# Layer-norm variance on GpSimd, and a different share of the depthwise convolution on TensorE, in a float32 transformer block

## The chip, the cores and the metric

The kernel runs on one core of a Trainium2 chip. The core has five engines that run side by side, each with its own queue of instructions: TensorE (PE in the profile; PEld is its loading of weights), VectorE (DVE), ScalarE (ACT), GpSimd (POOL) and SyncE (SP, used here to issue transfers). Transfers are carried out by 16 DMA engines; GpSimd, ScalarE and SyncE can issue them, and some transfers add to what lies at their target ("accumulating" transfers). The metric is the time of one execution on the device in microseconds (us).

## The reference, cut to what matters

The input is a batch of 16 images with 128 channels and 96 x 96 pixels, all in float32. One block of a Restormer-like network is computed: a layer norm over channels, attention between channels, a second layer norm, and a feed-forward part with a 3 x 3 depthwise convolution on 512 hidden channels.

```python
B, C, H, W = (16, 128, 96, 96)
HEADS = 8; HID = 4 * C; EPS = 1e-05

def _layernorm(x, w, b):
    mu = jnp.mean(x, axis=-1, keepdims=True)
    var = jnp.mean(jnp.square(x - mu), axis=-1, keepdims=True)
    return (x - mu) / jnp.sqrt(var + EPS) * w + b

def _ffn(xn_nchw, w_in, w_dw, w_out):
    h1 = einsum('bchw,oc->bohw', xn_nchw, w_in[:, :, 0, 0])
    h2 = conv_general_dilated(h1, w_dw, strides (1, 1), padding ((1, 1), (1, 1)), feature_group_count=HID)
    h3 = gelu(h2, approximate=False)
    return einsum('bchw,oc->bohw', h3, w_out[:, :, 0, 0])

xn1 = _layernorm(x_hwc, ln1_w, ln1_b)              # over the 128 channels of a pixel
x = x + attention(xn1, wq, wk, wv, wp)             # softmax over channels, 8 heads of 16
xn2 = _layernorm(x_hwc, ln2_w, ln2_b)
x = x + _ffn(xn2, w_in, w_dw, w_out)
```

## The kernel before

Channels lie on the 128 partitions, pixels along the free dimension. An image is cut into 8 bands of 12 rows (1152 pixels), a band into 3 units of 4 rows (384 pixels); there are 128 bands, numbered g. The 512 hidden channels are 4 chunks of 128, numbered n.

The order of instructions on every engine is fixed when the program is built. The kernel describes each operation with an engine, a place in time, its inputs and outputs and an estimated duration; a small planner then simulates the engines and writes the instructions down in the order in which they would start. The table `AT` shifts the place of each kind of operation, and so acts as a table of priorities.

```python
PE_CHUNK = 3
PE_BANDS = (0, 2, 4, 6, 8, 10)
PE_OF = 11
PE_LAST = (0, 1, 2, 4, 5, 7)
DMA_TAPS = (1, 2, 3)
QT, QB = 4, 1
X1_BUFS, XB_BUFS, PR_BUFS, H3_BUFS, ZT_BUFS = 2, 6, 5, 10, 3
AT = dict(weights=10.45, ..., stats_a=-5.05, variance_a=-7.4, power_a=-1.65, shift_a=-5.8, ...)
```

A layer norm over channels needs pixels on the partitions, so each group of four tiles of 128 pixels is transposed into a PSUM bank (two such banks, `p_tr`, take turns; at the start of the program other banks are used), and what follows happens there. The variance, the power and the shift work on 4 numbers per partition:

```python
def forth(q):                     # TensorE: 4 transposes into one PSUM bank
    ... nc.tensor.transpose(d["pT", q][:, k, :], xt[:, j * P : (j + 1) * P], ident)

def stats(j):                     # VectorE: mean and squared deviations, two tiles at a time
    nc.vector.bn_stats(d["st"][:, j, :], d["pT", qs[h]][:, k : k + 2, :].rearrange("p t c -> p c t"))

def variance():                   # 128 x 4
    nc.vector.tensor_scalar(ve, d["mv"][:, :, 2], 1.0 / C, EPS, ALU.mult, ALU.add)

def power():                      # GpSimd: (var + eps) ** -0.5, 128 x 4
    nc.gpsimd.tensor_tensor(rstd, d["ve"], mhalf, ALU.pow)

def shift():                      # VectorE: -mean * rstd, 128 x 4
    nc.vector.scalar_tensor_tensor(nb, d["mv"][:, :, 1], -1.0, d["rstd"], ALU.mult, ALU.mult)

def scaled(q):                    # ScalarE: normalised tile into SBUF, one per tile of 128 pixels
    nc.scalar.activation(zT(q)[:, k, :P], d["pT", q][:, k, :], AF.Identity, bias=nb, scale=rstd)
```

The first norm (`_a`) feeds the gram matrix of the channels on TensorE, from which attention is worked out; both norms then transpose back (`pB_a`, `pB_b`) and place the result in `xn`. An image has 72 tiles, or 18 groups of four, for each norm: 288 groups of the first norm and 288 of the second in the whole program.

The depthwise convolution is shared out. For a pair (g, n) in `jobs`, TensorE makes the hidden rows, ScalarE copies them out of PSUM and multiplies them for tap 0 and for two or three more taps, whose products are summed by accumulating transfers that GpSimd issues; VectorE does the other five or six taps, one instruction each over the whole band:

```python
def product(t):                   # ScalarE
    nc.scalar.activation(to, shifted(t), AF.Copy, scale=dw[:, n, t : t + 1])

def tap(t):                       # VectorE, 128 x 1152: two tensor inputs and a scalar
    nc.vector.scalar_tensor_tensor(h3, shifted(t), dw[:, n, t : t + 1], h3, ALU.mult, ALU.add)

def add_products(t):              # issued by GpSimd
    nc.gpsimd.dma_start(out=to, in_=d["pr", t], accum_op=ALU.add)
```

The fourth chunk (n = 3) of some bands is done by TensorE alone instead: the hidden layer's weights are multiplied into the nine taps (`comp`), and nine matmuls per unit add up in PSUM, three units to a band; then ScalarE applies the gelu. Which bands these are:

```python
def by_pe(g):
    k = NG - 1 - g
    return k in PE_LAST if k < NB else k % PE_OF in PE_BANDS

jobs += [(g, n) for n in range(NCH) if n != PE_CHUNK or not by_pe(g)]
```

At last `ffn_out` multiplies the four chunks with the output weights and VectorE adds the result to x. The weights themselves are transposed once, in the opening, at the place `weights`.

Of the kernel before, what the change touches and what calls it, by code (L numbers as in the profile page):

```python
# [11 lines left out]
ALU = mybir.AluOpType  # L12
# [4 lines left out]
EPS = 1e-5  # L17
UR = 4
BR = 12
PE_CHUNK = 3  # L20
PE_BANDS = (0, 2, 4, 6, 8, 10)
PE_OF = 11
PE_LAST = (0, 1, 2, 4, 5, 7)
TINY = 1e-20
DMA_TAPS = (1, 2, 3)
# [4 lines left out]
X1_BUFS, XB_BUFS, PR_BUFS, H3_BUFS, ZT_BUFS = 2, 6, 5, 10, 3  # L30
IN_TURN = ("tr", "h3", "pr", "xb", "x1")
AT = dict(
    weights=10.45, zeros=-0.55, load_a=-15.15, forth_a=-12.6, stats_a=-5.05, variance_a=-7.4,
    power_a=-1.65, shift_a=-5.8, scaled_a=-2.25, gram=-2.15, back_a=-19.55, place_a=-30,
    attention=-11.35, mix=-10.3, residual=-15.8, mixed=-15.6, add_x=2.25, forth_b=-11.95, stats_b=-3.7,
    variance_b=-5.4, power_b=-20.6, shift_b=-22.65, scaled_b=-2.4, back_b=-19.15, place_b=-0.55,
    halo=4.55, hidden=-1.65, kept=-8.9, product=-7.6, products=2.05, add_last=-4.65, tap=7.3,
    add_first=25.4, gelu=-4.85, conv=-0.8, conv_gelu=-6.2, out=2.3, add=7.1, store=-8.95,
)
STEP = dict(scaled=0.3, hidden=0.1, products=0.5, tap=0.166, conv=1.6, conv_tap=0.03, out=0.8, out_part=0.05)  # L40
SLACK = 300
NORM1_END = 6.0
EARLY = 5
WAIT = dict(POOL=350, SP=1300, ACT=1300)
T_WEIGHTS = 20000
T_POWER = 1000
T_ADD, T_MOVE = 3100, 1800


class Plan:  # L50
# [14 lines left out]
    def op(self, engine, ns, place, work, reads, writes, result, own=None, dma=0, two=False):  # L65

        k = len(self.ops)
        needs = {}
        for t in reads:
            if t in self.writer:
                needs[self.writer[t]] = True
        for t in writes:
            if t in self.writer:
                needs[self.writer[t]] = True
            for r in self.readers.get(t, ()):
                needs[r] = True  # L80
        for t in reads:
            self.readers.setdefault(t, []).append(k)
        new = []
        for t in writes:
            self.writer[t], self.readers[t] = k, []
            if t[0] in self.free and t[:2] not in self.users and t[:2] not in new:
                new.append(t[:2])
        for t in {t[:2]: None for t in (*reads, *writes)}:
            if t[0] in self.free:
                self.users.setdefault(t, []).append(k)  # L90
                needs[self.users[t][0]] = True
        needs.pop(k, None)
        self.ops.append((engine, ns, place, work, list(needs), new, result, own or result, dma, two))
# [111 lines left out]
def tile_restormer_block(  # L205
# [23 lines left out]
    nc = tc.nc  # L229
    B, C, H, W = x.shape  # L230
# [105 lines left out]
    op = plan.op  # L336

    def at(kind, place):
        return place + AT[kind]

    def bank(key, n=4 * P):

        return banks[plan.slot["h", key]][:, :n]
# [18 lines left out]
    def pe(ns, p, f, r, w):  # L362
        op("PE", ns, p, f, r, w, ns + 200 + SLACK, ns)

    def dve(ns, p, f, r, w, two=False):
        op("DVE", ns, p, f, r, w, ns + 120 + SLACK, ns + 120, two=two)
# [29 lines left out]
    def weights(p):  # L396
# [52 lines left out]

        op("ACT", 400, at("load_a", p), loads, [], mine, T_WEIGHTS, dma=2 * T_MOVE)  # L450
        dve(400, at("weights", p), shifts, [], [("w", "in"), ("w", "conv"), ("w", "shift")])
# [24 lines left out]
    def x_key(i, b, second):  # L476

        return "xb" if second or i == 0 and b < XB_BUFS else "x1"
# [14 lines left out]
    def norm(i, second, place_of):  # L493

        name = f"{'b' if second else 'a'}{i}"
        ab = "_b" if second else "_a"
        zTs = {}

        def xtok(u):
            return (x_key(i, u // UPB, second), (i, u // UPB), u % UPB)  # L500
# [34 lines left out]
        def pixels(s, m):  # L535

            d = {}
            qs = range(m * QB, (m + 1) * QB)
            early = i == 0 and (not second or m < EARLY)
            key_ = "h" if early else "tr"  # L540
            by_dve = QT // 2 if early else 0

            def forth(q):
                if early:
                    d["pT", q] = bank((name, q)).rearrange("p (t c) -> p t c", c=P)
                else:
                    d["pT", q] = p_tr.tile([P, QT, P], F32, tag="tr", name=f"pT_{name}_{q}")
                for k in range(QT):
                    b, j = divmod(q * QT + k, TPB)
                    xt = (xbs if x_key(i, b, second) == "xb" else x1s)[i, b]  # L550
                    nc.tensor.transpose(d["pT", q][:, k, :], xt[:, j * P : (j + 1) * P], ident)  # L551

            def stats(j):

                if j == 0:
                    d["st"] = small.tile([P, QB * QT // 2, 6], F32, tag="st", name=f"st_{name}_{m}")
                h, k = divmod(2 * j, QT)
                nc.vector.bn_stats(
                    d["st"][:, j, :], d["pT", qs[h]][:, k : k + 2, :].rearrange("p t c -> p c t")
                )  # L560

            def variance():
                d["mv"] = d["st"].rearrange("p j (t v) -> p (j t) v", v=3)
                ve = d["ve"] = small.tile([P, QB * QT], F32, tag="ve", name=f"ve_{name}_{m}")
                nc.vector.tensor_scalar(ve, d["mv"][:, :, 2], 1.0 / C, EPS, ALU.mult, ALU.add)  # L565

            def power():
                rstd = d["rstd"] = small.tile([P, QB * QT], F32, tag="rstd", name=f"rstd_{name}_{m}")
                nc.gpsimd.tensor_tensor(rstd, d["ve"], mhalf, ALU.pow)  # L569

            def shift():
                nb = d["nb"] = small.tile([P, QB * QT], F32, tag="nb", name=f"nb_{name}_{m}")
                nc.vector.scalar_tensor_tensor(nb, d["mv"][:, :, 1], -1.0, d["rstd"], ALU.mult, ALU.mult)  # L573

            def zT(q):
                zTs[q] = zT_bufs[plan.slot["zT", (name, q)]]
                return zTs[q]

            def also_scaled(q):
                for k in range(by_dve):  # L580
                    t = (q - qs[0]) * QT + k
                    nc.vector.tensor_scalar(
                        zT(q)[:, k, :P], d["pT", q][:, k, :], d["mv"][:, t, 1:2], d["rstd"][:, t : t + 1],
                        ALU.subtract, ALU.mult,
                    )

            def scaled(q):
                for k in range(by_dve, QT):
                    t = (q - qs[0]) * QT + k
                    nc.scalar.activation(  # L590
                        zT(q)[:, k, :P], d["pT", q][:, k, :], AF.Identity,
                        bias=d["nb"][:, t : t + 1], scale=d["rstd"][:, t : t + 1],
                    )

            def gram(q):
                if q == 0:
                    grams[i] = p_g.tile([P, 4 * P], F32, tag="g", name=f"g_{i}")
                for k in range(QT):
                    zt = zTs[q][:, k, :]
                    nc.tensor.matmul(  # L600
                        grams[i][:, : P + 1], lhsT=zt[:, :P], rhs=zt,
                        start=(q == 0 and k == 0), stop=(q == NU * TPU // QT - 1 and k == QT - 1),
                    )

            trs, bt = [(key_, (name, q)) for q in qs], ("batch", (name, m))
            for q, tr in zip(qs, trs):
                units = {t // TPU: None for t in range(q * QT, (q + 1) * QT)}
                pe(110 * QT, at("forth" + ab, s), lambda q=q: forth(q), [xtok(u) for u in units], [tr])
            for j in range(QB * QT // 2):
                dve(341, at("stats" + ab, s), lambda j=j: stats(j), [trs[2 * j // QT]], [bt])  # L610
            dve(80, at("variance" + ab, s), variance, [], [bt])
            op("POOL", T_POWER, at("power" + ab, s), power, [], [bt], T_POWER + 33 + SLACK)
            dve(80, at("shift" + ab, s), shift, [], [bt])
            for h, (q, tr) in enumerate(zip(qs, trs)):
                zt, sh = ("zT", (name, q)), s + STEP["scaled"] * h
                if by_dve:
                    dve(by_dve * 240, at("scaled" + ab, sh), lambda q=q: also_scaled(q), [tr, bt], [(*zt, 0)])
                act((QT - by_dve) * 343, at("scaled" + ab, sh), lambda q=q: scaled(q), [tr, bt], [(*zt, 1)])
                if not second:
                    pe(QT * 220, at("gram", sh), lambda q=q: gram(q), [(*zt, 0), (*zt, 1), ("w", "ones")], [("g", i)])  # L620
# [315 lines left out]
# [4 lines that stand above are left out]
# [59 lines left out]
```

## Time and profile before

| | before |
|---|---|
| time, median of 3 | 4335.04 us (4330.35 to 4336.72) |
| span of the profiled execution | 4333.3 us |
| busy: PE, DVE, ACT, POOL | 4279.2, 4196.3, 4125.7, 1935.5 us |
| mean busy share of the 16 DMA engines, 100 to 4200 us | 0.89 |
| VectorE taps (L840) | 2578 |
| TensorE passes of the convolution (L891) | 3888 |
| powers on GpSimd (L569) | 576 |
| first tap starts at | 95.8 us |

A row of a group in the profile names the line of the kernel, the engine, the operation, what it writes and reads with shapes, and how often it occurs; behind the bar stand the busy time in us and the mean duration of one in ns, then the idle time of the engine just before such instructions and what ended most of it. A float32 matmul is recorded as two passes. Records of pipelined instructions overlap, so the spacing of their starts can be shorter than a duration. Line 569 is the power, 565 the variance, 573 the shift, 558 the statistics, 590 the scaling, 840 a tap, 836 a product, 891 the convolution on TensorE, 820 the hidden layer, 914 the output, 509 the mix of attention, 921 the last addition.

### The profile page before, as it was taken

The page shows a single profiled execution, that of the slowest core. Times are in us where ns is not written, and L with a number is a line of the kernel's source. Part 1 is how long each engine was busy: PE and PEld are TensorE (multiplying, and loading weights), DVE is VectorE, ACT ScalarE, POOL GpSimd, SP SyncE. Part 2 cuts the span into 40 slices and gives each one's busy share as a digit, 9 for nine tenths or more (in the row PEclk, how much of TensorE's full clock was granted, in tenths as well). Part 3 has the DMA queues.
Part 4 walks back from the last instruction along what each step waited for, and adds up shares of the span by engine and source line. Part 5 has one row for each costly group of instructions (what it writes and reads, how often), then busy time and mean ns, then how long its engine had stood idle before and what let it go on. Part 6 is the DMA issues. An engine that isn't in the chain of part 4 may idle for free.

```text
span 4333.3 us, 53606 instructions
## 1 busy us (share of the span) xinstructions
PE 4279.2 (99%) x17734; PEld 2732.2 (63%) x17734; DVE 4196.3 (97%) x5626; ACT 4125.7 (95%) x7232; POOL 1935.5 (45%) x1721
## 2 busy tenths in 40 slices
PE   8999999999999999999999999999999999999999
PEld 6666666666665666666666666666666666666565
DVE  6999999999999999999999999999999999999998
ACT  5999999999999999999999999999999999999996
POOL 3444454444454444444445444544444444444331
PEclk9999999999999999999999999999999999999999
DMA  2898898888988889899888988888989898888896
GB/s 85 171 187 186 178 191 182 184 185 185 189 188 185 184 179 194 175 192 190 175 186 179 192 180 182 187 183 181 193 176 194 173 194 187 179 190 170 178 191 145
DMA packets 193001, 782.89 MB, mean 181 GB/s; under 512 B 22355, under 2 KB 23763, under 8 KB 192723
## 3 DMA queue, kind: packets, MB, share of 16 engines
q0 software_dynamic: 153216, 627.64, 76.7%
q1 hardware_dynamic: 37152, 151.01, 9.6%
q8 instruction: 141, 2.31, 0.2%
q10 hardware_dynamic: 2352, 0.81, 0.1%
q14 instruction: 140, 1.12, 0.1%
HBM read 148.26 MB, written 75.50 MB: 52 GB/s over the span
## 4 chain that ended last, share of the span: by engine, by line
PE 40%; DVE 21%; ACT 15%; DMA 5%; issue 4%; POOL 2%; POOLq 0%; DVEq 0%; ACTq 0%
DVE h L840 17%; PE h L891 13%; PE h L914 9%; PE h L820 8%; ACT pr L836 4%; ACT zT L590 3%; DMA h<-pr 3%; ACT h L825 2%; PE g L600 2%; PE h L509 2%; ACT h L836 2%; ACT h L848 2%; DMA pr<-pr 1%; PE pT_b L551 1%; PE pB_b L630 1%
## 5 line engine op out<-in xcount | busy, mean ns | idle before, releaser
L840 DVE SCALAR_TENSOR_TENSOR h<-h,dw,h 128x1152 f32<-128x1152 f32 x2578 | 3570.2, 1409 | 15.5 <-ACT h L836 11.0
L891 PE MATMUL h<-xn,comp 128*128 128x384 f32 x3888 | 1409.4, 487 | 1.4 <-DVE x L921 0.9
L836 ACT ACTIVATE pr<-h,dw 128x1152 f32<-128x1152 f32 x942 | 1287.4, 1389 | 6.8 <-DMA pr<-pr 6.6
L914 PE MATMUL h<-h,woutT 128*128 128x384 f32 x3072 | 1144.4, 488 | 4.6 <-ACT x L518 1.6
L820 PE MATMUL h<-xn,winT 128*128 128x384 f32 (+1 forms) x2640 | 1043.5, 501 | 5.7 <-ACT x L518 3.2
L891 PEld LDWEIGHTS h<-xn,comp 128*128 128x128 f32 x3888 | 705.6, 190 | 424.4 <-issue 10.0
L825 ACT COPY h<-h 128x384 f32<-128x384 f32 (+1 forms) x1320 | 732.4, 604 | 62.7 <-PE h L820 50.8
L844 POOL DMA_DIRECT2D pr<-pr x503 | 462.7, 921 | 700.5 <-ACT pr L836 533.0
L914 PEld LDWEIGHTS h<-h,woutT 128*128 128x128 f32 x3072 | 556.5, 190 | 335.9 <-issue 6.4
L844 POOL DMA_DIRECT2D h<-pr x439 | 413.1, 941 | 780.6 <-DVE h L840 129.2
L569 POOL TENSOR_TENSOR rstd_a<-ve_a,mhalf 128x4 f32<-128x4 f32 x288 | 504.6, 1758 | 370.3 <-DVE ve_a L565 340.3
L569 POOL TENSOR_TENSOR rstd_b<-ve_b,mhalf 128x4 f32<-128x4 f32 x288 | 526.8, 1830 | 303.9 <-DVE ve_b L565 292.2
L820 PEld LDWEIGHTS h<-xn,winT 128*128 128x128 f32 x2640 | 473.4, 190 | 295.7 <-issue 39.2
L836 ACT ACTIVATE h<-h,dw 128x1152 f32<-128x1152 f32 x440 | 600.1, 1365 | 4.4 <-PE h L914 2.2
L848 ACT ACTIVATE h<-h 128x1152 f32<-128x1152 f32 (+1 forms) x442 | 562.9, 1274 | 34.7 <-DMA h<-pr 32.6
L590 ACT ACTIVATE zT<-pT_b,nb_b,rstd_b 128x128 f32<-128x128 f32 x1132 | 456.5, 577 | 2.4 <-DVE nb_b L573 1.9
L590 ACT ACTIVATE zT<-pT_a,nb_a,rstd_a 128x128 f32<-128x128 f32 x1080 | 445.9, 612 | 6.9 <-DVE nb_a L573 6.8
L600 PEld LDWEIGHTS g<-zT 128*128 128x128 f32 x2304 | 297.8, 192 | 61.7 <-issue 11.1
L600 PE MATMUL g<-zT 128*128 128x129 f32 x2304 | 305.1, 275 | 0.0
L509 PE MATMUL h<-xn,mwT 128*128 128x384 f32 x768 | 289.0, 489 | 5.3 <-ACT h L825 2.1
L634 ACT ACTIVATE xn<-pB_b,b 128x384 f32<-128x384 f32 x384 | 274.1, 714 | 10.7 <-PE pB_b L630 10.7
L636 ACT COPY xn<-pB_a 128x384 f32<-128x384 f32 x384 | 243.3, 634 | 23.6 <-PE pB_a L630 23.2
(145 smaller groups left out, 3375.6 us busy)
## 6 DMA issues: line engine op xcount, KB each, us to landing
pr<-pr POOLq DMA_DIRECT2D x503, 576.0 KB, 6.2
h<-pr POOLq DMA_DIRECT2D x439, 576.0 KB, 6.4
x<-in_x_dram SPq DMA_DIRECT2D x128, 576.0 KB, 5.9
out_dram<-x SPq DMA_DIRECT2D x127, 576.0 KB, 4.5
x<-in_x_dram POOLq DMA_DIRECT2D x122, 576.0 KB, 7.1
out_dram<-x SPq DMA_DIRECT2D x3, 192.0 KB, 1.8
weights<-in_L_conv_w_in_dram ACTq DMA_DIRECT2D x1, 256.0 KB, 11.0
weights<-in_L_conv_w_out_dram ACTq DMA_DIRECT2D x1, 256.0 KB, 11.8
```

Source lines behind the costliest of these rows:

```text
L509: nc.tensor.matmul(rows(pm), lhsT=mats[i][0], rhs=interior(i, u), start=True, stop=True)
L569: nc.gpsimd.tensor_tensor(rstd, d["ve"], mhalf, ALU.pow)
L590: nc.scalar.activation(zT(q)[:, k, :P], d["pT", q][:, k, :], AF.Identity, bias=d["nb"][:, t : t + 1], scale=d["rstd"][:, t : t + 1],)
L600: nc.tensor.matmul(grams[i][:, : P + 1], lhsT=zt[:, :P], rhs=zt, start=(q == 0 and k == 0), stop=(q == NU * TPU // QT - 1 and k == QT - 1),)
L820: nc.tensor.matmul(rows(ph), lhsT=winT[:, n, :], rhs=window(xn, r0 + r, e - r, 1), start=True, stop=True)
L825: nc.scalar.copy(window(h1_, r, e - r, 1), rows(d.pop(("ph", r))))
L836: nc.scalar.activation(to, shifted(t), AF.Copy, scale=dw[:, n, t : t + 1])
L840: nc.vector.scalar_tensor_tensor(h3, shifted(t), dw[:, n, t : t + 1], h3, ALU.mult, ALU.add)
L844: nc.gpsimd.dma_start(out=to, in_=d["pr", t], accum_op=ALU.add)
L848: nc.scalar.activation(h3, h3, AF.Gelu)
L891: nc.tensor.matmul(d["pc"], lhsT=comp[:, t, :], rhs=window(xn, r0 + dy, UR, dx), start=(t == 0), stop=(t == 8),)
L914: nc.tensor.matmul(rows(d["po"]), lhsT=woutT[:, n, :], rhs=h3s[g, n][:, s * UR : (s + 1) * UR, :], start=(k == 0), stop=(k == NCH - 1),)
```

## The change

Three things change. The variance of the layer norm moves from VectorE to GpSimd, directly ahead of the power that reads it there, so that VectorE is relieved of a small instruction per group. The bands whose fourth chunk TensorE convolves are now every other one instead of six of eleven; in the last image they stay six of eight. And the table of priorities is a different one; in it the weight transposes have a later place (11.05 for 10.45) and the first norm's loads and transposes an earlier one. Buffer numbers, tiles and arithmetic stay.

```diff
-PE_BANDS = (0, 2, 4, 6, 8, 10)
-PE_OF = 11
+PE_BANDS = (0,)
+PE_OF = 2
 PE_LAST = (0, 1, 2, 4, 5, 7)
...
 AT = dict(
-    weights=10.45, zeros=-0.55, load_a=-15.15, forth_a=-12.6, stats_a=-5.05, variance_a=-7.4,
-    power_a=-1.65, shift_a=-5.8, scaled_a=-2.25, gram=-2.15, back_a=-19.55, place_a=-30,
-    ...
+    weights=11.05, zeros=-2.3, load_a=-22.85, forth_a=-15, stats_a=-11, variance_a=-7.95, power_a=3.5,
+    shift_a=-15.95, scaled_a=-2.85, gram=-4.15, back_a=-20.9, place_a=-21.85, attention=-18.15, mix=-8.5,
+    ...
 )
...
+T_VARIANCE = 420
 T_POWER = 1000
...
-                nc.vector.tensor_scalar(ve, d["mv"][:, :, 2], 1.0 / C, EPS, ALU.mult, ALU.add)
+                nc.gpsimd.tensor_scalar(ve, d["mv"][:, :, 2], 1.0 / C, EPS, ALU.mult, ALU.add)
...
-            dve(80, at("variance" + ab, s), variance, [], [bt])
+            op("POOL", T_VARIANCE, at("variance" + ab, s), variance, [], [bt], T_VARIANCE + 33 + SLACK)
             op("POOL", T_POWER, at("power" + ab, s), power, [], [bt], T_POWER + 33 + SLACK)
             dve(80, at("shift" + ab, s), shift, [], [bt])
```

The numbers T_... are the durations, in ns, that the planner assumes.

More of the change, by code (lines that the diff above doesn't have):

```diff
@@ L32 @@
 AT = dict(
-    weights=10.45, zeros=-0.55, load_a=-15.15, forth_a=-12.6, stats_a=-5.05, variance_a=-7.4,
-    power_a=-1.65, shift_a=-5.8, scaled_a=-2.25, gram=-2.15, back_a=-19.55, place_a=-30,
[L35 to L38, printed above, removed]
+    weights=11.05, zeros=-2.3, load_a=-22.85, forth_a=-15, stats_a=-11, variance_a=-7.95, power_a=3.5,
+    shift_a=-15.95, scaled_a=-2.85, gram=-4.15, back_a=-20.9, place_a=-21.85, attention=-18.15, mix=-8.5,
+    residual=-15.95, mixed=-8.45, add_x=12.05, forth_b=-12.4, stats_b=-8.15, variance_b=-11.85,
+    power_b=-15.9, shift_b=-27.4, scaled_b=2.2, back_b=-22.2, place_b=-0.25, halo=6.25, hidden=0.55,
+    kept=-7.05, product=-12.5, products=4.05, add_last=-15.5, tap=1.25, add_first=23.45, gelu=-16.4,
+    conv=-0.5, conv_gelu=-14.15, out=3.65, add=-2.4, store=-0.9,
 )
```

## The prediction

> **What bounds the kernel now.** I read the busy shares first, then the chain of work that ended last, then the costliest groups, then the timeline of single engines, to turn durations into occupancy. The page gives the shares and the chain by engine:
>
> ```profile
> PE 4279.2 (99%) x17734; PEld 2732.2 (63%) x17734; DVE 4196.3 (97%) x5626; ACT 4125.7 (95%) x7232; POOL 1935.5 (45%) x1721
> ...
> PE 40%; DVE 21%; ACT 15%; DMA 5%; issue 4%; POOL 2%; POOLq 0%; DVEq 0%; ACTq 0%
> DVE h L840 17%; PE h L891 13%; PE h L914 9%; PE h L820 8%; ACT pr L836 4%; ACT zT L590 3%; DMA h<-pr 3%; ACT h L825 2%; PE g L600 2%; PE h L509 2%; ACT h L836 2%; ACT h L848 2%; DMA pr<-pr 1%; PE pT_b L551 1%; PE pB_b L630 1%
> ```
>
> Three engines are above 95%, and the end hangs on all three in turn, TensorE most. So no single busy share decides; what matters is how much work each engine really has. A record's duration contains a tail that overlaps the next instruction, so I use spacing. The chain shows it, because there each piece lasts until the next begins. The longest run of taps, and a few pieces between 2000 and 2100 us:
>
> ```profile
> 1330.43 15.95 DVE h L840 x12
> ```
>
> ```profile
> 2007.08 1.15 ACT pr L836
> 2008.23 1.05 ACT h L848
> ...
> 2041.32 1.40 ACT zT L590 x4
> ...
> 2058.56 2.58 PE h L914 x8
> ```
>
> One VectorE tap occupies 15.95/12 = 1.329 us (its record says 1.409). One pass of a 384-column matmul occupies 2.58/8 = 0.3225 us, and a float32 product is two passes: 0.645 us. A ScalarE product occupies 1.15, a gelu of a band 1.05, one scaled tile 0.35. With the counts of the groups:
>
> ```profile
> L840 DVE SCALAR_TENSOR_TENSOR h<-h,dw,h 128x1152 f32<-128x1152 f32 x2578 | 3570.2, 1409 | 15.5 <-ACT h L836 11.0
> L891 PE MATMUL h<-xn,comp 128*128 128x384 f32 x3888 | 1409.4, 487 | 1.4 <-DVE x L921 0.9
> L569 POOL TENSOR_TENSOR rstd_a<-ve_a,mhalf 128x4 f32<-128x4 f32 x288 | 504.6, 1758 | 370.3 <-DVE ve_a L565 340.3
> ```
>
> TensorE: conv 3888 x 0.3225 = 1254; output 3072 x 0.3225 = 991; hidden layer 440 jobs x 1.975 = 869 (a job has on average 12.25 rows of 96, or 3.06 times 384 columns, at 0.645); mix 768 x 0.3225 = 248; 4608 transposes x 0.11 = 507; gram 2304 x 0.111 = 256; attention and setup about 50. Sum **4174**, 96% of 4333. VectorE: 2578 x 1.329 = 3426; 1152 statistics x 0.34 = 392; 384 output adds x 0.47 = 180; variance and shift 1152 x 0.07 = 81; rest about 60. Sum **4139**, 95.5%. ScalarE by the same method is near **4060**, 94%. The gap of the largest sum to the span is 4333 - 4174 = 159 us; about 95 us of the span is the opening, before the first tap starts at 95.76.
>
> **The small instructions** need a closer look. VectorE and GpSimd near 2009 us:
>
> ```profile
> 2008.79 0.16 DVE L573 SCALAR_TENSOR_TENSOR nb_b<-st_b,rstd_b 128x4 f32<-128x4 f32 x1
> 2008.86 0.16 DVE L565 TENSOR_SCALAR ve_a<-st_a 128x4 f32<-128x4 f32 x1
> 2008.93 2.74 DVE L840 SCALAR_TENSOR_TENSOR h<-h,dw,h 128x1152 f32<-128x1152 f32 x2
> ```
>
> ```profile
> 2009.18 2.06 POOL L569 TENSOR_TENSOR rstd_a<-ve_a,mhalf 128x4 f32<-128x4 f32 x1 [0.21 <-DVE ve_a L565]
> ```
>
> The variance has a record of 0.16 us, but the next instruction starts 0.07 us after it: 0.07 is what removing it gives back. The power starts at 2009.18, a quarter of a microsecond into a tap, and ends at 2011.24. The tap ended near 2010.34, so the power ran 0.9 us after the tap let go. Over the whole trace, 434 of 576 powers start inside a tap, and their median end is 0.896 us after that tap's end; the minimum of 0.996 us is a power with no tap in its way. The taps themselves are not stretched (1389 to 1428 ns, all 2578).
>
> **What the Trainium skill says.** "SBUF — State Buffer", section "Who interferes with whom": a VectorE instruction with two SBUF inputs contends with a GpSimd instruction that reads SBUF, because its second input comes through the shared read interface. The taps and the power are such a pair, and the trace agrees: the power waits for the tap's end. The page also says that whoever starts first holds the pair for its whole instruction. Here the trace differs: the next tap starts on time while the power computes for 0.9 us. "Perfetto Trace Analysis", section "Optimizing Scalar/DVE Operations", warns that offloading between VectorE and GpSimd might not help because of that shared port, and says a recorded latency is about twice the engine's busy time for such small work; 0.16 recorded against 0.07 spacing agrees. The same page, "Identifying the Most-Contended Engine", says that matmul busy time is not a fair measure of headroom; agreed, 99% busy is 96% by spacing.
>
> **The change part by part.** *Convolution.* Of the 120 bands outside the last image, 66 were on TensorE by the rule "six of eleven"; now every other one is, 60. The last image keeps six. So 72 becomes 66, and 6 jobs of chunk 3 go to ScalarE, VectorE and DMA. TensorE loses 6 x 27 x 0.645 = 104.5 us and gains 6 x 1.975 = 12 of hidden layer: **-92.6**, to 4081. VectorE gains 6 jobs x 6 taps x 1.329 = **+47.8** (chunk 3 never has the third DMA tap). ScalarE gains per job three products 3.45, gelu 1.05, three copies of 0.375 and a halo row of about 0.22, 5.85 us, x 6 = 35, and loses 18 small gelus at 0.38 = 7: **+28**, to about 4090. DMA gets 12 more accumulating transfers beside 942. The software queue's 76.7% of 4333 us over 1064 transfers is 3.12 us each, so +37 us, to about 78%: hidden, unless they arrive late.
>
> *Variance.* VectorE loses 576 x 0.07 = **-40.3**. Together with the taps it has +7.5: **4147**. GpSimd gets 576 small instructions of an estimated 0.3 us when free, estimated from the power's 1.0. In steady state each also reads SBUF and will mostly wait for a tap. When it is done the next tap has begun, and the power waits for that one too. So statistics to reciprocal root get one more tap, **+1.3 us** per group of four tiles: 576 x 1.3 = 750 us of GpSimd span, from 45% to some 62%, waiting and not computing. What leaves a second wait on VectorE is the shift; it waits for the power 67 times now, 58 us in all.
>
> *Setup and priorities.* The weight transposes are 20 passes, under 4 us of TensorE, and lie in the opening. The changed table of priorities reorders everything, with buffer numbers kept. I take both as zero in themselves, and as the means to place the longer wait behind other work.
>
> *Sum.* The largest occupancy falls from 4174 (TensorE) to 4147 (VectorE), 27 us. With the same gap of 159: 4306. TensorE is no longer level with VectorE, which takes some waits away (the statistics and output adds wait some 29 us for TensorE now); the longer normalisation chain gives some back. I call it **4308**.
>
> **Rivals.** *Transpose buffers become the bound.* Two PSUM buffers carry a group from its transposes to the fourth scaled tile. Pairing starts and ends in order over the trace gives a mean of 12.63 us (first norm) and 12.11 (second) for 553 groups, or 3419 us per buffer, 79% of the span. With 1.3 us more that is about 3780, 88%. For it: bunching then leaves TensorE and ScalarE waiting. Against it: 4.6 to 5.0 us of the hold lies behind the shift, where the scaling waits its turn on ScalarE, and can shrink. It would make about 4350 to 4370. *TensorE alone set the pace.* It has the largest share of the chain, so all 92 us could come: 4240 to 4250. Against it: VectorE would have to run at 4147/4245, 97.7%, opening included. *GpSimd delays the accumulating DMAs.* They are issued in order behind the waiting variance. The gelu waits 32.6 us for them now; doubled, and with later buffers, about 4340. For it: the DMA engines are 88% busy already. Against it: GpSimd idles over half the span.
>
> **Range and chances.** The sums bound the gain at about 90 us (TensorE's whole relief), and the two waiting rivals cost 30 to 60. I give half the chance to 4290 to 4325. The range that should hold it eight times in ten is **4270 to 4350**. Two per cent is 87 us: faster by that needs the whole relief (0.04), slower needs the buffers to jam (0.03), within 2% 0.93.
>
> **What would show it.** Right: conv matmul records 3564, taps 2614, tap spacing still 1.33; TensorE's busy share a few points lower while VectorE's is level or higher; VectorE's share of the chain up; the power still ending 0.9 us after a tap; statistics to shift, now 4.1 us in the mean, near 5.4. Wrong: a variance on GpSimd that waits for no tap or lasts over a microsecond alone; taps stretched by it; idle time before the shift far above 58 us; transposes waiting for scaled tiles much more often; a first tap well away from 96 us. The prediction falls if the gap of 159 us is not a property of three crowded engines, but of one of them.

## The result and the profile after

The changed kernel takes 4314.84 us (median of 6, 4313.11 to 4320.11) against 4333.42 for the kernel before on the same chip: a ratio of 0.9958, 95% interval 0.9945 to 0.9971. The prediction was 4308 us and "within 2%".

The page of the kernel after, the line of busy shares and the lines of the chain:

```profile
PE 4216.3 (98%) x17446; PEld 2686.8 (62%) x17446; DVE 4190.5 (97%) x5086; ACT 4149.9 (96%) x7256; POOL 2427.5 (56%) x2309
...
PE 46%; ACT 32%; DVE 13%; DMA 4%; issue 3%; POOL 2%; ACTq 0%; POOLq 0%; DVEq 0%
PE h L915 13%; PE h L892 12%; DVE h L841 10%; PE h L821 9%; ACT pr L837 8%; ACT zT L591 6%; ACT h L826 4%; ACT h L837 4%; ACT h L849 4%; DMA h<-pr 4%; PE g L601 3%; PE h L510 2%; ACT x L519 2%; PE pB_a L631 1%; ACT xn L635 1%
```

Line numbers are one higher than before. TensorE is 63 us less busy and GpSimd 492 us more; VectorE hardly moved, because the taps that it gained replace the variances that it lost. The chain went to ScalarE and TensorE, not to VectorE. So the busy shares moved as the sums said, and the chain did not: VectorE's share of it, forecast to rise, fell from 21% to 13%.

The groups that answer to those shown of before:

```profile
L841 DVE SCALAR_TENSOR_TENSOR h<-h,dw,h 128x1152 f32<-128x1152 f32 x2614 | 3593.6, 1407 | 2.8 <-ACT h L837 1.2
L892 PE MATMUL h<-xn,comp 128*128 128x384 f32 x3564 | 1284.7, 487 | 3.5 <-DVE x L922 2.5
...
L570 POOL TENSOR_TENSOR rstd_a<-ve_a,mhalf 128x4 f32<-128x4 f32 x288 | 497.0, 1726 | 13.5 <-POOL ve_a L566 0.2
L566 POOL TENSOR_SCALAR ve_b<-st_b 128x4 f32<-128x4 f32 x288 | 298.2, 1035 | 326.9 <-DVE st_b L559 321.3
```

The counts are 2614 taps and 3564 passes, as worked out. The second norm's variance on GpSimd has a mean of 1035 ns (both norms: 1015) for an instruction on 4 numbers per partition. GpSimd's timeline near 2007 us shows what that is:

```profile
2006.61 1.28 POOL L566 TENSOR_SCALAR ve_a<-st_a 128x4 f32<-128x4 f32 x1
2007.97 2.09 POOL L570 TENSOR_TENSOR rstd_a<-ve_a,mhalf 128x4 f32<-128x4 f32 x1
```

and VectorE's timeline for the same time:

```profile
2006.09 0.42 DVE L559 BATCH_NORM_STATS2 st_a<-pT_a 128x6 f32<-128x256 f32 x1
2006.43 4.06 DVE L841 SCALAR_TENSOR_TENSOR h<-h,dw,h 128x1152 f32<-128x1152 f32 x3
2010.41 0.15 DVE L574 SCALAR_TENSOR_TENSOR nb_a<-st_a,rstd_a 128x4 f32<-128x4 f32 x1
```

The first of three taps starts at 2006.43 and ends near 2007.8; the variance starts inside it and ends at 2007.89. The power starts inside the second tap, which ends near 2009.2, and ends at 2010.06. The shift follows after the third tap. The chain waits for a tap twice, as predicted, and the shift is three taps behind the statistics.

Now sums by spacing, for both kernels. Work is the count of each group times the median spacing from its instruction to the next on that engine; waiting is what the single spacings exceed these medians by, added up. Shapes of one line have to be kept apart. The hidden layer before, for one, has two:

```profile
L820 PE MATMUL h<-xn,winT 128*128 128x384 f32 x2224 | 857.9, 488 | 4.7 <-ACT x L518 2.3 <-DVE x L921 1.0 <-ACT h L897 0.9
L820 PE MATMUL h<-xn,winT 128*128 128x480 f32 x416 | 196.8, 568 | 1.0 <-ACT x L518 0.8 <-DVE x L921 0.2
```

The median spacing of the first is 0.325 us and of the second 0.404 us.

| | before: work, waiting | after: work, waiting |
|---|---|---|
| TensorE | 4225, 116 | 4133, 185 |
| VectorE | 4185, 157 | 4193, 127 |
| ScalarE | 4043, 273 | 4086, 223 |

The largest work falls by 32 us, from TensorE's 4225 to VectorE's 4193. What is left of the span beside it, called the rest below, is 109 us before (4333 - 4225) and 119 after (4312 - 4193).

### The profile page after: what moved, and what is told of

Read it like the earlier page. It is cut to its first block, busy times and chain, and to the rows that moved or that the text cites. A ratio compares the mean times of both kernels' runs of the same rounds, so it can differ in the third digit from the quotient of the medians.

```text
span 4311.6 us, 52468 instructions
## 1 busy us (share of the span) xinstructions
PE 4216.3 (98%) x17446; PEld 2686.8 (62%) x17446; DVE 4190.5 (97%) x5086; ACT 4149.9 (96%) x7256; POOL 2427.5 (56%) x2309
## 4 chain that ended last, share of the span: by engine, by line
PE 46%; ACT 32%; DVE 13%; DMA 4%; issue 3%; POOL 2%; ACTq 0%; POOLq 0%; DVEq 0%
PE h L915 13%; PE h L892 12%; DVE h L841 10%; PE h L821 9%; ACT pr L837 8%; ACT zT L591 6%; ACT h L826 4%; ACT h L837 4%; ACT h L849 4%; DMA h<-pr 4%; PE g L601 3%; PE h L510 2%; ACT x L519 2%; PE pB_a L631 1%; ACT xn L635 1%
## 5 line engine op out<-in xcount | busy, mean ns | idle before, releaser
L892 PE MATMUL h<-xn,comp 128*128 128x384 f32 x3564 | 1284.7, 487 | 3.5 <-DVE x L922 2.5
L892 PEld LDWEIGHTS h<-xn,comp 128*128 128x128 f32 x3564 | 653.3, 189 | 430.7 <-issue 27.1
L845 POOL DMA_DIRECT2D pr<-pr x509 | 480.5, 944 | 521.0 <-ACT pr L837 434.1
L826 ACT COPY h<-h 128x384 f32<-128x384 f32 (+1 forms) x1338 | 712.2, 588 | 39.0 <-PE h L821 26.2
L845 POOL DMA_DIRECT2D h<-pr x445 | 427.7, 963 | 562.7 <-DVE h L841 139.9
L821 PEld LDWEIGHTS h<-xn,winT 128*128 128x128 f32 x2676 | 485.9, 190 | 333.8 <-issue 28.4
L849 ACT ACTIVATE h<-h 128x1152 f32<-128x1152 f32 x448 | 561.8, 1254 | 32.1 <-DMA h<-pr 28.4
L570 POOL TENSOR_TENSOR rstd_b<-ve_b,mhalf 128x4 f32<-128x4 f32 x288 | 513.8, 1784 | 11.8
L566 POOL TENSOR_SCALAR ve_b<-st_b 128x4 f32<-128x4 f32 x288 | 298.2, 1035 | 326.9 <-DVE st_b L559 321.3
L566 POOL TENSOR_SCALAR ve_a<-st_a 128x4 f32<-128x4 f32 x288 | 286.2, 994 | 291.5 <-DVE st_a L559 287.5
```

Source lines behind the costliest of these rows:

```text
L566: nc.gpsimd.tensor_scalar(ve, d["mv"][:, :, 2], 1.0 / C, EPS, ALU.mult, ALU.add)
L821: nc.tensor.matmul(rows(ph), lhsT=winT[:, n, :], rhs=window(xn, r0 + r, e - r, 1), start=True, stop=True)
L826: nc.scalar.copy(window(h1_, r, e - r, 1), rows(d.pop(("ph", r))))
L849: nc.scalar.activation(h3, h3, AF.Gelu)
L892: nc.tensor.matmul(d["pc"], lhsT=comp[:, t, :], rhs=window(xn, r0 + dy, UR, dx), start=(t == 0), stop=(t == 8),)
```

## The experiments

The change has three parts: bands, variance, table. All eight combinations were run, then versions that keep one order of instructions and change only what is executed. My theory is the one of the prediction: the engine with the largest sum of work sets the time, with 159 us on top. Its rivals: TensorE alone set the pace; the table (the order) made the gain; the longer chain over GpSimd costs.

### One part alone, and all but one

Bands alone, `bands_only`:

```diff
-PE_BANDS = (0, 2, 4, 6, 8, 10)
-PE_OF = 11
+PE_BANDS = (0,)
+PE_OF = 2
```

> The kernel before with every other band convolved on TensorE and nothing else changed. If the largest sum of occupancy sets the time (VectorE then has 4139 + 48 = 4187 us of work, and 159 us of gap are added): 4346 us, ratio 1.003. If TensorE's relief of 93 us alone brought the gain: about 4315, ratio 0.996. If the table of priorities brought it: 4333 or above.

Measured: 4394.33 us, ratio 1.0147 (1.0133 to 1.0161). The bands alone make the kernel slower. TensorE's relief is worth nothing where VectorE gets 48 us more to do; the rival that TensorE alone set the pace falls. The direction is that of the largest sum, but the loss is 63 us (against 4331.37 for the kernel before in the same set) and not 13. Its page:

```profile
PE 4242.6 (97%) x17446; PEld 2680.3 (61%) x17446; DVE 4236.0 (96%) x5662; ACT 4150.1 (94%) x7256; POOL 1952.5 (44%) x1733
```

VectorE is busy 40 us more than before (48 by spacing) and still only 96% of a span that grew by 59.

Variance alone, `var_only` (the two lines of the variance as in the change):

> The kernel before with the variance on GpSimd and nothing else changed. Largest sum: TensorE keeps 4174 us, so 4333, ratio 1.000. VectorE sets the pace: its 40 us come, about 4293, ratio 0.991. The longer chain from statistics to shift costs: 4340 to 4360.

Measured: 4341.86 us, ratio 1.0027 (1.0015 to 1.0038). VectorE has 40 us less work and the kernel is no faster, but slightly slower: TensorE is still the fullest engine (4222 us by spacing, against VectorE's 4146).

Table alone, `table_only` (`AT` of after in the kernel before):

> The kernel before with the table of priorities of after and nothing else changed. Largest sum: no engine has less work, so 4333, ratio 1.000. If the order of instructions brought the gain: about 4315, ratio 0.996. If a table only suits the shares of work it was chosen for: slower, 4345 to 4380.

Measured: 4347.98 us, ratio 1.0041 (1.0029 to 1.0054). The table is not a gain by itself. Its opening is 8.5 us longer (first tap at 104.3 us), its end 8 us shorter (7.8 us from the start of the last tap to the end, against 15.8).

All but the variance, `after_var_dve`:

```diff
-                nc.gpsimd.tensor_scalar(ve, d["mv"][:, :, 2], 1.0 / C, EPS, ALU.mult, ALU.add)
+                nc.vector.tensor_scalar(ve, d["mv"][:, :, 2], 1.0 / C, EPS, ALU.mult, ALU.add)
-            op("POOL", T_VARIANCE, at("variance" + ab, s), variance, [], [bt], T_VARIANCE + 33 + SLACK)
+            dve(80, at("variance" + ab, s), variance, [], [bt])
```

> The kernel after with the variance back on VectorE. Largest sum: VectorE has 4187 us, so 4346, ratio to before 1.003. If moving the variance does nothing: 4315, ratio 0.996. If the longer chain on GpSimd costs more than the 40 us of VectorE bring: below 4315.

Measured: 4360.44 us, ratio 1.0071 (1.0058 to 1.0083). It seems to say that the move is worth 46 us, about the 40 of VectorE's relief. The runs that keep one order, below, show that this reading is wrong.

All but the bands, `after_old_bands` (six of eleven):

> The kernel after with the six-of-eleven bands of before. Largest sum: TensorE has 4174 us again, so 4333, ratio to before 1.000. If TensorE's relief does nothing: 4315, ratio 0.996. If VectorE sets the pace, its 48 us fewer of taps make it faster than after: about 4270 to 4300.

Measured: 4345.28 us, ratio 1.0025 (1.0016 to 1.0034).

All but the table, `after_old_table`:

> The kernel after with the table of priorities of before. Largest sum: the same work as after, 4147 + 159 = 4306, ratio to before 0.994. If the table brought the gain: 4333, ratio 1.000. If a table suits only the shares of work it was chosen for: above 4333.

Measured: 4331.72 us, ratio 0.9994 (0.9986 to 1.0003). The same work as after, in another order, gives nearly the whole gain away.

Against the largest sum plus 159:

| | expected | measured | over | largest work by spacing | rest of the span |
|---|---|---|---|---|---|
| bands_only | 4346 | 4394 | 48 | VectorE 4233 | 159 |
| var_only | 4333 | 4342 | 9 | TensorE 4222 | 118 |
| table_only | 4333 | 4348 | 15 | TensorE 4222 | 126 |
| after_var_dve | 4346 | 4360 | 14 | VectorE 4233 | 128 |
| after_old_bands | 4333 | 4345 | 12 | TensorE 4222 | 120 |
| after_old_table | 4306 | 4332 | 26 | VectorE 4193 | 144 |
| after | 4306 | 4315 | 9 | VectorE 4193 | 119 |

Every mixture lies above its sum plus 159. The last two columns take the work from the trace instead. With six of eleven bands TensorE is the fullest engine, and the rest stays near the 109 us of before: 118 to 126. With every other band VectorE is the fullest, and the rest goes from 119 to 159.

Only all three parts together are faster: the bands cost 1.5% on the kernel before and bring 0.7% (1.0025 to 0.9958) where the variance and the table are already there. But each mixture is also planned anew and so has another order, and the runs below show that the order alone moves the time by 29 and 43 us. So these differences can't be put down to the parts themselves.

### How much a small change of order does

`after_w_place`: the weight transposes' place at 10.45, as before, in the kernel after.

> The kernel after with the place of the weight transposes at 10.45 as before, instead of 11.05, all other priorities as after. If the place of the transposes matters, the first tap starts some us earlier or later than 96.0 us and the end follows by as much. If it only reshuffles the opening: within 3 us of 4315. A difference larger than the shift of the first tap shows how much a small change of order alone moves the time.

Measured: 4319.85 us, ratio 0.9964 (0.9951 to 0.9978). The interval overlaps that of after; the first tap starts at 96.0 us in both. In the traces every engine executes the same sequence of instructions in both kernels, by line, names and shapes. So this place changed nothing in the order, and the run is in effect a repeat of after: 5 us is what two measurements of one order can differ by. The place of the weight transposes has no part in the gain.

`after_no_var`: no variance at all, planned without one. The power reads the statistics directly, so the division by 128 and the epsilon are left out.

```diff
-            op("POOL", T_VARIANCE, at("variance" + ab, s), variance, [], [bt], T_VARIANCE + 33 + SLACK)
...
-                nc.gpsimd.tensor_tensor(rstd, d["ve"], mhalf, ALU.pow)
+                nc.gpsimd.tensor_tensor(rstd, d["mv"][:, :, 2], mhalf, ALU.pow)
```

> The kernel after without the variance instruction: the power reads the sum of squared deviations itself, so the division by 128 and the epsilon are left out of what is computed. If the instruction on GpSimd costs nothing (VectorE's and TensorE's sums are unchanged): 4315, ratio to before 0.996. If its wait lengthens the hold of the transpose buffers at a cost: 4295 to 4305.

Measured: 4336.43 us, ratio 1.0000 (0.9992 to 1.0008). An instruction less, and 22 us slower than after. None of the stated theories expected this. It led to the next runs, in which the order stays and only the executed instruction changes.

### The same order, another instruction

In the next three runs the traces show on TensorE, VectorE and ScalarE, apart from the variance, the same sequence of instructions as in the kernel that each was made from. Medians of different sets of runs are compared as they stand; where they give 22, 29 and 43 us, the ratios to the kernel before, timed beside each, give 18, 27 and 45.

`after_silent_var`: the planner still allots the variance its 420 ns on GpSimd, but it is not written out (the same part of the computation is left out as in `after_no_var`).

> The kernel after, in its own order of instructions, but the variance instruction is not written out: the planner still allots its 420 ns, and the power reads the sum of squared deviations, so the division by 128 and the epsilon are left out of what is computed. If the instruction on GpSimd is hidden: 4315 us, ratio to before 0.996. If its wait costs: 4295 to 4308. If the earlier run without a variance was slow for its order alone, this one is faster than its 4336.

Measured: 4307.03 us, ratio 0.9938 (0.9925 to 0.9950). It executes the same instructions as `after_no_var`, in another order, and is 29 us faster. Against after, the variance on GpSimd seems to cost about 8 us; the two intervals just overlap, so that is not clearly shown.

`before_silent_var`: the kernel before in its own order, its variance on VectorE not written out.

> The kernel before, in its own order, with the variance instruction on VectorE not written out (division and epsilon left out as above). VectorE loses 40 us. If TensorE's occupancy sets the time: 4333, ratio 1.000. If VectorE's does: about 4293, ratio 0.991.

Measured: 4321.12 us, ratio 0.9974 (0.9965 to 0.9984). Of the 40 us that VectorE no longer has to do, 11 reach the end.

`after_order_var_dve`: the kernel after, with one word changed, so that the variance runs on VectorE in an order planned for GpSimd.

```diff
-                nc.gpsimd.tensor_scalar(ve, d["mv"][:, :, 2], 1.0 / C, EPS, ALU.mult, ALU.add)
+                nc.vector.tensor_scalar(ve, d["mv"][:, :, 2], 1.0 / C, EPS, ALU.mult, ALU.add)
```

> The kernel after in its own order, with only the engine of the variance changed back to VectorE (the planner still thinks it is on GpSimd). If VectorE's occupancy sets the time after the change: 40 us more, about 4355, ratio to before 1.005, near the 4360 of the version that was planned for VectorE. If the shorter chain outweighs this: below 4330.

Measured: 4317.47 us, ratio 0.9968 (0.9956 to 0.9979), an interval that overlaps that of after. VectorE has 41 us more work (4234 by spacing), and the time is not measurably different. It is also 43 us faster than `after_var_dve`, which executes the same operations on the same engines. So those 43 us lie in the order. The waits of VectorE in three kernels show where it waits less. The columns are the total, how often, and the longest. First after:

```profile
DVE nb_a L574 <- POOL rstd_a L570: 27.9, 31, 2.0
DVE nb_b L574 <- POOL rstd_b L570: 25.6, 27, 2.0
```

`after_order_var_dve`, the order of after:

```profile
DVE nb_b L574 <- POOL rstd_b L570: 15.4, 17, 0.9
DVE nb_a L574 <- POOL rstd_a L570: 11.3, 13, 1.1
```

`after_var_dve`, planned for VectorE:

```profile
DVE nb_b L574 <- POOL rstd_b L570: 29.6, 31, 2.3
DVE nb_a L574 <- POOL rstd_a L570: 26.4, 32, 2.4
```

In after and `after_order_var_dve` the shift stands 2.99 taps behind the last statistics, in the mean of 576 groups; in `after_var_dve` 2.72; before 2.52; in `after_no_var` 1.93. The planner leaves this room because it thinks a variance on GpSimd takes 420 ns and a tap's end. When the variance then runs on VectorE, the room is spare: against `after_var_dve` the wait for the power falls to 27 us from 56, and all of VectorE's recorded waits to 79 from 115. TensorE's fall to 84 from 109. The other pair says the same: `after_no_var`

```profile
DVE nb_b L575 <- POOL rstd_b L571: 30.4, 31, 2.4
DVE nb_a L575 <- POOL rstd_a L571: 28.9, 38, 0.9
```

and `after_silent_var`, the same instructions in the order of after:

```profile
DVE nb_a L572 <- POOL rstd_a L568: 18.1, 21, 0.9
DVE nb_b L572 <- POOL rstd_b L568: 14.7, 16, 0.9
```

59 us against 33. The traces of these two pairs differ by 34 us (4330.2 and 4295.7) and 45 us (4361.5 and 4316.2); 26 and 29 of these stand on VectorE before the shift. That tells where VectorE waits less. It does not show that the room is the cause, and one run speaks against the room alone: `after_old_table` has as much of it, 3.02 taps, executes the same work as after, is 17 us slower, and still waits 60 us there:

```profile
DVE nb_a L574 <- POOL rstd_a L570: 33.7, 34, 2.0
DVE nb_b L574 <- POOL rstd_b L570: 26.8, 27, 2.0
```

### Levelling the engines further

`after_63_bands`: ten of nineteen bands on TensorE.

```diff
-PE_BANDS = (0,)
-PE_OF = 2
+PE_BANDS = (0, 2, 4, 6, 8, 10, 12, 14, 16, 18)
+PE_OF = 19
```

> The kernel after with ten of nineteen bands on TensorE (63 of 120) instead of every other one (60), which levels the two engines: VectorE 24 us less, TensorE 46 us more, both near 4125 us by spacing. By the largest sum and the same gap: about 4290, ratio to before 0.990. If level engines wait for one another more, or the table suits only its own shares: 4310 to 4345.

Measured: 4344.85 us, ratio 1.0034 (1.0021 to 1.0046). The sums became level (TensorE 4178, VectorE 4170 by spacing), and the waiting on VectorE rose from 127 to 189 us; the shift alone waits 73. The level share of work, under a table that was kept, was worse, not better, by 30 us.

## Why the prediction was right, and where its steps were off

**The shares of work: right.** By median spacing TensorE fell by 92 us (predicted 92.6) and VectorE rose by 8 (7.5). ScalarE rose by 43 (28): with the spacings of before its added instructions come to 28, and the others lie mostly in the copies out of PSUM, whose median spacing went from 0.359 to 0.370 us. The software queue went to 78.0% (78%). The marginal 0.07 us of a small VectorE instruction held, not its record of 0.16.

**"The largest occupancy falls by 27 us, with the same gap": near in size, and partly by luck.** The largest work fell by 32 us and the rest of the span grew by 10, which makes the 22 us between the two traces; the medians differ by 19. Both sums of the prediction were too low, TensorE's 4174 by 51 us and VectorE's 4139 by 46. The hidden layer takes 891 us and not 869, since 208 of its 1320 products are 480 columns wide (a job has 12.47 rows in the mean, not 12.25), and the small instructions at the end of each sum take 81 and 104 us, not 50 and 60. As both were short by about the same, the difference survived; the gap was taken 50 us too wide.

That the gap stayed was luck. It is not a property of three crowded engines, which the prediction named as its weak point. With VectorE the fullest it went from 82 us (`after_order_var_dve`) to 159 (`bands_only`), and the same work under the table of before takes 4332 us, where the prediction took the table as zero. Nor is the sum plus 159 a floor: the mixtures lay 9 to 48 us above it and 63 bands 59 (4345 against 4127 + 159), but `after_order_var_dve` lies 29 us below it (4317 against 4346) and `before_silent_var` 12 (4321 against 4333). The gap belongs to the order.

**"VectorE loses 40.3 us": true on the engine, nearly nothing at the end.** In the order of after, the variance on VectorE or GpSimd makes no measurable difference. With it on VectorE, VectorE's work is 41 us more and its waiting 37 less (127 to 90), 27 of them at the shift. So the relief is mostly paid back there. In the order of before, 11 of 40 us reached the end when the variance was left out. What the move brought beside this is another order, with more room ahead of the shift; that this room is what helps is not shown.

**"One tap more, +1.3 us": too large.** Statistics to shift went from 4.04 to 4.62 us, +0.6. The variance on VectorE had not been free either: it started 1.00 us behind the statistics, queued behind a tap, where on GpSimd it starts after 0.41. The variances take 584 us of GpSimd and not 750, for two reasons: 107 of the 576 started between taps and took under 0.4 us, and one that starts inside a tap waits only for what is left of it, where the prediction charged a full tap. GpSimd's busy time rose by 492 us, less than 584, mostly because records on it overlap.

**The transposes' buffers: right in sum by luck, and harmless.** They are held 3807 us each (predicted about 3780). But the prediction added 1.3 us to every group, and the first norm's mean hold fell from 12.63 to 12.11 us while the second's rose from 12.11 to 15.35. Yet TensorE's weight loads wait less for scaled tiles in the two transposes, 31 us against 47 before. The hold has slack in it, as argued. "GpSimd delays the accumulating transfers" did not come: the gelu waits 28.4 us for them, 32.6 before.

**The opening and setup: zero, as taken.** The first tap starts at 96.0 us against 95.8. The prediction left out the end: with the table of after the last tap starts 7.8 us before the end and not 15.8. That this is worth 8 of the 19 us is not shown, since `table_only` and `after_no_var` have the same end and are not faster than before.

**What stays open.** Whether the kernel before would gain from more planned room alone (a larger assumed duration of the power) was not tried, and neither was a table fitted to 63 bands. That the time hangs on the order is shown by two pairs of runs, by 29 and 43 us; what in the order does it is not settled, since the room at the shift differs in both pairs but does not set `after_old_table` apart from after. Whether moving the variance brings as little in other orders is open too. Why `bands_only` lies 48 us above its sum is not settled; its gelus wait 57.2 us for the accumulating transfers, against 32.6 before and 28.4 after.

## What to carry to other kernels

Sum the work of each engine by spacing of starts, not by recorded duration, and keep shapes apart. The largest sum bounds the time from below, but what comes on top is no constant: here 82 to 173 us. Relieving one of several nearly level engines may bring nothing, or go with a loss, as in `bands_only`. Where a program fixes the order, separate the instruction from the order: keep the order and change only the engine, or leave the instruction out of an order that still reserves it. A comparison of two planned versions charges the planner's luck and its assumed latencies to the instruction, here 43 us of an apparent 46. A repeat of the same order differed by 5 us.

## What the runs showed of the hardware that was not expected

GpSimd can miss the gap between taps. Its timeline in the kernel after near 2000 us:

```profile
1999.27 3.93 POOL L566 TENSOR_SCALAR ve_b<-st_b 128x4 f32<-128x4 f32 x1 [1.37 <-DVE st_b L559]
2003.29 1.03 POOL L570 TENSOR_TENSOR rstd_b<-ve_b,mhalf 128x4 f32<-128x4 f32 x1
```

and VectorE's:

```profile
1999.09 4.06 DVE L841 SCALAR_TENSOR_TENSOR h<-h,dw,h 128x1152 f32<-128x1152 f32 x3
2004.35 0.17 DVE L574 SCALAR_TENSOR_TENSOR nb_b<-st_b,rstd_b 128x4 f32<-128x4 f32 x1 [1.20 <-POOL rstd_b L570]
```

Three taps ran back to back from 1999.09 to 2003.15, and the variance ended only after the third, at 2003.20; the shift then waited 1.20 us. Of 576 variances 11 took more than 2.4 us. A variance that meets no tap takes 0.18 us at the least.
